# A bank for each head's scores and a raised priority for the operation that empties it, in a conv, scan and attention kernel

## The chip, the cores and the metric

The kernel runs on one core of one Trainium2 chip. A core has five engines, each with its own queue of instructions: TensorE (PE, matmuls; its weight loads are shown apart as PEld), VectorE (DVE), ScalarE (ACT), GpSimd (POOL) and SyncE (SP), which here issues most of the DMAs. PE writes its results to PSUM[...]. The metric is the device time of one execution in microseconds; the number given is the median of several runs.

## What is computed

The reference has two layers on an input of 8 images of 384 channels and 32 x 32 points (1024 tokens). Layer 0 is a normalisation, a Mamba block run forwards and backwards (a selective scan with 16 states per channel), and a gated local 3x3 convolution. Layer 1 is causal attention with six heads of 64 and a feed-forward with quantised activations. Cut to what matters:

```python
# layer 0, for both directions, and a local convolution
u = silu(conv1d(x @ in_proj)); dt, Bm, Cm = split(u @ x_proj)
delta = softplus(dt @ dt_proj + bias)
h = exp(delta * A) * h + (delta * u) * Bm        # the scan, 16 states
y = (h * Cm).sum() + u * D;  out = (y * silu(z)) @ out_proj
local = sigmoid(conv3x3(xn) + b) * xn
x = x + res_scale * (scale * (out_fwd + out_bwd) + local)
# layer 1
scores = einsum('bhqd,bhkd->bhqk', q, k); scores = where(causal, scores, -inf)
t = t + (softmax(scores) @ v) @ Wproj + bproj
t = t + ffn(layernorm(t))                        # with 8-bit quantisation by groups of images
```

The quantisation has five groups of one image each (8 images divided by five, rounded down); what lies outside the groups stays zero. So the feed-forward is computed for images 0 to 4 alone.

## The kernel before

Every tile has 128 channels or tokens on the partitions; the 384 channels are three blocks, the 1024 tokens two halves of 512, one bank each. The stages of one image are these.

- before_scan: normalisation, in projection (L341), the 1D convolution (taps on DVE at L369 for the first image, as matmuls with diagonal weights at L371 for later ones), the local convolution (`loc`, L389 and nine taps on DVE at L400), the SiLU (L434), the x projection (L487), and the "delta" step (L518 to L528: a matmul, four ACT and four DVE operations), whose results go to DRAM and are loaded again.
- The scan. It is cut into 768 units, 96 per image, of two states and 512 tokens each. For a unit POOL multiplies `g = ud * bc` (L588), ACT makes two decays `da` in PSUM (L601), DVE runs two scans (L606), POOL copies a carry (L611) and multiplies by the second row (L612), and PE transposes and adds the result into the bank `y` (L620). `g` has six buffers; POOL's first product is issued two units ahead.
- attention: projections, then for each of three pairs of heads and each block of 128 queries `scores` (below), then the transposes of the probabilities (L862), the product with the values (L875) and the rescaling (L833 to L839), and the output projection (L934).
- feed_forward: two matrix products (L992, L1036) with GELU and quantisation.

What an engine does in which order is fixed when the program is built. The scheduling layer takes the instructions in program order as their priority, gives each tile a buffer when its first instruction is placed, and puts on each engine's queue the instruction with the best priority whose inputs, by its own estimate of times, are ready. `tc.high_priority(offset=n)` gives the instructions within it a priority as if they stood n places earlier. `pin` keeps an instruction in program order on its engine. Two lists set the program order: the first image's stages alone, then slots of the scan with the preparation of the next three images spread beside them (the lists `first` and `beside`, L1121 to L1144), and after that the scan's slots with attention and feed-forward of the images done, spread by estimated durations (L1146 to L1168). The last image's attention comes at the end, alone.

Banks are tiles with a tag. `BANKS` gives each tag its number of banks, eight in all; `bank(name, tag)` takes a tile of a tag, and without a tag takes "s" and "pt" in turn (`turn`). The tag "s" has two banks. Its users are the scores, but also the preparation of the first four images (tags "s" and "pt" in turn), the projections of attention by the turn, and the feed-forward.

A pair of heads has its scores in two banks. The matmul of head 1 is issued first, that of head 0 right after it at a high priority; each uses 64 rows of the array. For each head DVE then adds the causal mask, negates, and finds the minimum along the row (L800, "the mask" below; a second short record reads the accumulated minimum `nm`), and ACT takes the exponential with `nm` as bias (L810).

Of the kernel before, what the change touches and what calls it, by code (L numbers as in the profile page):

```python
# [12 lines left out]
ALU = mybir.AluOpType  # L13
# [24 lines left out]
MASKED = -1e30  # L38
# [16 lines left out]
def kernel(  # L55
# [16 lines left out]
    nc = tc.nc  # L72
# [17 lines left out]
    def mtile(name, n=L):  # L90
        return mid.tile([P, n], F32, name=name, tag="mid")
# [1 line left out]

    BANKS = {"y": 1, "da": 2, "s": 2, "pt": 2, "av": 1}
    turn = [0]

    def bank(name, tag=None):
        if tag is None:  # L100
            turn[0] += 1
            tag = ("s", "pt")[turn[0] % 2]
        return ps.tile([P, HB], F32, name=name, tag=tag, bufs=BANKS[tag])

    def half(h):
# [2 lines left out]
    def chunk(c):  # L108
        return slice(c * P, (c + 1) * P)
# [29 lines left out]
    for d in range(2):  # L139
        nc.scalar.dma_start(out=wdt[d * DW : d * DW + RANK, :], in_=w_dt)  # L140
        nc.scalar.dma_start(
            out=wdt[d * DW + RANK : d * DW + RANK + 1, :],
# [53 lines left out]
    def binarize(src, dst, nk, nout, per, name, emit):  # L196
# [15 lines left out]
        @emit  # L212
        def _():
            st["mps"] = bank(f"mps_{name}", "av")
# [44 lines left out]
    def mean_of(c_of, name):  # L259

        m = bank(name)
        for c in range(NC):
            nc.tensor.matmul(out=m, lhsT=onesc, rhs=c_of(c), start=(c == 0), stop=(c == NC - 1))
        return m
# [42 lines left out]
    def before_scan(b, tags, emit, later=None, diags=None):  # L307
# [5 lines left out]
        def bank_of(name):  # L313
            return bank(name, next(turns))
# [359 lines left out]
    def attention(b, emit_ffn, emit):  # L674
# [83 lines left out]
        def at_once(second):  # L758
            return tc.high_priority(offset=HURRY) if second else nullcontext()

        def rows_of(e):
            return slice(e * HD, (e + 1) * HD)

        def blocks_of(n):
            return [(k0, min(k0 + HB, n)) for k0 in range(0, n, HB)]

        def probabilities(c, g, steps):


            nb = g + 1  # L770

            def scores(i, qi, n, kb, k0, k1):
                pr = mtile(f"pr_{b}_{c}_{qi}_{kb}").rearrange("p (e l) -> p e l", e=2)
                st["pr", c, g, i, kb] = pr
                if kb == 0 and i == 0:
                    for what in ("nm", "rs"):
                        st[what, c, g] = small.tile(
                            [P, QT, 2, nb], F32, name=f"{what}_{b}_{c}_{g}", tag=f"{what}{nb}"
                        )
                nm, rs = st["nm", c, g], st["rs", c, g]  # L780
                ss = [bank(f"s_{b}_{c}_{qi}_{kb}_{e}", "s") for e in range(2)]

                order = (1, 0)
                for e in order:
                    with at_once(e == order[1]):
                        mm = nc.tensor.matmul(  # L786
                            out=ss[e][:, : k1 - k0],
                            lhsT=st["q"][rows_of(e), c, chunk(qi)],
                            rhs=st["k"][rows_of(e), c, k0:k1],
                            start=True,  # L790
                            stop=True,
                        )
                    if e == order[1]:
                        pin(mm)

                w = k1 - k0
                mask = cmask[:, HB - w :] if k1 == n else cmask[:, :1].to_broadcast([P, w])
                for e in range(2):
                    x, m = pr[:, e, :w], nm[:, i, e, kb : kb + 1]
                    nc.vector.tensor_tensor_reduce(  # L800
                        out=x,
                        in0=ss[e][:, :w],
                        in1=mask,
                        scale=-1.0,
                        scalar=-MASKED,
                        op0=ALU.add,
                        op1=ALU.min,
                        accum_out=m,
                    )
                    nc.scalar.activation(  # L810
                        x, x, AF.Exp, bias=m, scale=-1.0, accum_out=rs[:, i, e, kb : kb + 1]
                    )

            for i in range(QT):
                qi = g * QT + i
                n = (qi + 1) * P
                for kb, (k0, k1) in enumerate(blocks_of(n)):
                    steps(lambda i=i, qi=qi, n=n, kb=kb, k0=k0, k1=k1: scores(i, qi, n, kb, k0, k1))
# [402 lines left out]
```

## Time and profile before

| | |
|---|---|
| median of 3 runs | 5041.66 us (5039.27 to 5051.98) |
| the profiled execution | 5052.48 us, span 5050.7 us, granted PE clock 0.883 |
| first scan of unit 0 / of unit 95 | 135.3 us / 774.3 us |
| last image's attention alone | from about 4838 us to the end |
| POOL: products L588 and L612 | 1837.9 and 1819.4 us |
| DVE: scans L606 | 907.7 and 955.1 us |
| DVE: masks L800, 576 | 298.9 us |
| PE: scores L786 | 394.6 us |

Busy time per engine in stretches of the span (us):

| stretch | PE | DVE | ACT | POOL |
|---|---|---|---|---|
| 0 to 135 | 56.05 | 89.61 | 64.39 | 13.95 |
| 135 to 215 | 47.25 | 79.38 | 48.16 | 24.07 |
| 215 to 700 | 375.02 | 395.05 | 287.76 | 378.28 |
| 700 to 840 | 100.25 | 124.68 | 81.63 | 102.13 |
| 840 to 4740 | 3212.96 | 2800.18 | 2059.06 | 3131.87 |
| 4740 to 4838 | 81.79 | 50.90 | 27.69 | 39.61 |
| 4838 to 5050 | 199.22 | 65.48 | 98.75 | 0.00 |

A profile is of one execution. In a line of instructions stand the source line, the engine, the operation, the tile written and the tiles read, and the count; an idle time is that of the engine just before the instruction, and the name behind the arrow is what ended it. A weight load and a matmul can run at the same time, so their idle times overlap too.

### The profile page before, as it was taken

The numbers are of one execution on the slowest core, as the hardware profiler recorded it, in microseconds if no ns is written. First come the engines' busy times: TensorE is split into PE (matmuls) and PEld (weight loads), VectorE is DVE, ScalarE is ACT, GpSimd is POOL, SyncE is SP. The second block draws the span as 40 slices with busy tenths as digits, with TensorE's granted clock in tenths as the row PEclk, the third lists the DMA queues.
The fourth block names the chain that finished last, engine by engine and source line by source line (L and its number), as shares of the span: only waits on it lengthen the run. The fifth ranks groups of instructions, "written<-read, shape, count | busy, mean of one in ns | idle before, by whom it ended". The sixth has DMA issues, their size and how long they took to land. (4 is left out here: it accounts for less than half of the span.)

```text
span 5050.7 us, 50731 instructions
## 1 busy us (share of the span) xinstructions
PE 4072.5 (81%) x16458; PEld 2180.7 (43%) x16458; DVE 3605.3 (71%) x4775; ACT 2667.4 (53%) x4850; POOL 3689.9 (73%) x1944
## 2 busy tenths in 40 slices
PE   4687787888888888788788888887787978978899
PEld 1243343444444444344444444443454444444444
DVE  6887988676887767786778867688766666676623
ACT  4565664564554655545656446555465355464426
POOL 0578687896868976778876688867788988888700
PEclk7788797989889889888999889998898989989999
DMA  6554546323453334463334633334533334334210
GB/s 227 204 175 160 200 155 229 109 88 118 152 187 135 119 115 154 139 200 111 103 134 143 213 111 128 110 123 155 194 132 106 118 108 143 109 101 139 88 58 26
DMA packets 365009, 696.35 MB, mean 138 GB/s; under 512 B 30104, under 2 KB 88904, under 8 KB 364744
## 3 DMA queue, kind: packets, MB, share of 16 engines
q1 hardware_dynamic: 355232, 676.97, 40.0%
q10 hardware_dynamic: 9512, 16.15, 0.9%
q8 instruction: 130, 2.13, 0.2%
q14 instruction: 135, 1.11, 0.1%
HBM read 527.33 MB, written 165.68 MB: 137 GB/s over the span
## 5 line engine op out<-in xcount | busy, mean ns | idle before, releaser
L588 POOL TENSOR_TENSOR g<-ud,bc 128x1024 f32<-128x1024 f32 x768 | 1837.9, 2393 | 654.0 <-PE y L620 523.0
L612 POOL TENSOR_TENSOR g<-g,bc 128x1024 f32<-128x1024 f32 x768 | 1819.4, 2369 | 194.9 <-DVE g L606 132.4
L601 ACT ACTIVATE da<-dl,amat 128x512 f32<-128x512 f32 x1536 | 1055.9, 691 | 1515.1 <-DVE g L606 1489.8
L606 DVE TENSOR_TENSOR_SCAN g<-da,g 128x512 f32<-128x512 f32 x768 | 907.7, 1210 | 509.6 <-POOL g L588 496.3
L606 DVE TENSOR_TENSOR_SCAN g<-da,carry,g 128x512 f32<-128x512 f32 x768 | 955.1, 1271 | 403.9 <-POOL g L588 374.5
L620 PE MATMUL y<-ident,g 128*128 128x128 f32 x6144 | 920.6, 297 | 210.3 <-POOL g L612 122.3
L620 PEld LDWEIGHTS y<-ident,g 128*128 128x128 f32 x6144 | 766.9, 153 | 644.3 <-issue 345.5
L786 PE MATMUL s<-k,q 64*128 64x512 f32 (+3 forms) x1152 | 394.6, 602 | 134.6 <-DVE nm L800 113.5
L800 DVE CUSTOM_DVE_ANT_0 pr<-s,cmask 128x512 f32<-128x512 f32 (+3 forms) x576 | 298.9, 544 | 179.3 <-PE s L786 159.9
L810 ACT ACTIVATE pr<-pr,nm 128x512 f32<-128x512 f32 (+3 forms) x576 | 348.4, 606 | 125.1 <-DVE nm L800 123.5
L862 PE MATMUL pt<-ident,pr 128*128 128x128 f32 x1728 | 302.1, 304 | 83.5 <-ACT ptn L864 38.5
L992 PE MATMUL hp<-t,w 128*128 128x512 f32 x720 | 339.3, 618 | 25.4 <-DMA w<-w1s 21.2
L1036 PE MATMUL yp<-h,w 128*128 128x512 f32 x720 | 331.9, 620 | 32.0 <-DMA w<-w2s 27.6
L341 PE MATMUL in<-xn,win 128*128 128x512 f32 x576 | 291.2, 651 | 36.5 <-DVE xc L463 15.9
L862 PEld LDWEIGHTS pt<-ident,pr 128*128 128x128 f32 x1728 | 207.0, 152 | 243.5 <-ACT ptn L864 94.3
L875 PE MATMUL av<-ptn,v 128*64 128x512 f32 (+3 forms) x1152 | 274.3, 559 | 23.2 <-DVE o L889 17.2
L611 POOL COPY carry<-g 128x2 f32<-128x2 f32 x384 | 87.7, 228 | 271.2 <-DVE g L606 271.2
L864 ACT COPY ptn<-pt 128x512 f32<-128x512 f32 (+3 forms) x576 | 254.7, 473 | 55.5 <-PE pt L862 53.5
L725 PE MATMUL qp<-t,wqk 128*128 128x512 f32 x576 | 267.8, 616 | 14.7 <-DVE t L302 12.5
L400 DVE SCALAR_TENSOR_TENSOR loc<-xn,vec,loc 128x496 f32<-128x496 f32 (+3 forms) x384 | 259.5, 722 | 20.3 <-ACT loc L389 19.0
L786 PEld LDWEIGHTS s<-k,q 64*128 64x128 f32 x1152 | 134.8, 206 | 266.5 <-DVE nm L800 190.1
L1036 PEld LDWEIGHTS yp<-h,w 128*128 128x128 f32 x720 | 141.9, 201 | 204.7 <-issue 177.2
(153 smaller groups left out, 4753.4 us busy)
## 6 DMA issues: line engine op xcount, KB each, us to landing
bc<-rows SPq DMA_DIRECT2D x512, 512.0 KB, 4.1
dl<-sdl SPq DMA_DIRECT2D x160, 256.0 KB, 2.9
ud<-sud SPq DMA_DIRECT2D x160, 256.0 KB, 2.7
t<-st SPq DMA_DIRECT2D x63, 512.0 KB, 5.1
su<-u SPq DMA_DIRECT2D x48, 512.0 KB, 3.6
du<-su SPq DMA_DIRECT2D x96, 256.0 KB, 3.8
sdl<-du SPq DMA_DIRECT2D x96, 256.0 KB, 2.9
sud<-du SPq DMA_DIRECT2D x96, 256.0 KB, 2.7
```

Source lines behind the costliest of these rows:

```text
L341: nc.tensor.matmul(out=mp, lhsT=st["win", c][:, k, i, :], rhs=st["xn"][:, k, half(h)], start=(k == 0), stop=(k == NC - 1),)
L588: pin(nc.gpsimd.tensor_tensor(g, ud, sst["bc", 0, u.b, u.part, u.n], ALU.mult))
L601: nc.scalar.activation(da, sst["dl", u.b, u.c, u.part], AF.Exp, scale=amat[:, u.c, n : n + 1])
L606: nc.vector.tensor_tensor_scan(gi[:, ::step], da[:, ::step], gi[:, ::step], first, ALU.mult, ALU.add)
L612: pin(nc.gpsimd.tensor_tensor(g, g, sst["bc", 1, u.b, u.part, u.n], ALU.mult))
L620: nc.tensor.matmul(out=y[:, j, :], lhsT=g[:, i, chunk(j)], rhs=ident, is_transpose=True, start=(u.opens and i == 0 and j == 0), stop=(u.cl ...
L786: mm = nc.tensor.matmul(out=ss[e][:, : k1 - k0], lhsT=st["q"][rows_of(e), c, chunk(qi)], rhs=st["k"][rows_of(e), c, k0:k1], start=True, st ...
L800: nc.vector.tensor_tensor_reduce(out=x, in0=ss[e][:, :w], in1=mask, scale=-1.0, scalar=-MASKED, op0=ALU.add, op1=ALU.min, accum_out=m,)
L810: nc.scalar.activation(x, x, AF.Exp, bias=m, scale=-1.0, accum_out=rs[:, i, e, kb : kb + 1])
L862: nc.tensor.transpose(pt[:, chunk(i)], pr[:, e, chunk(j % QT)], ident)
L992: nc.tensor.matmul(out=hp, lhsT=st["w1"][:, c, chunk(m % 2)], rhs=st["xn"][:, c, half(h)], start=(c == 0), stop=(c == NC - 1),)
L1036: nc.tensor.matmul(out=yp, lhsT=st["w2", k // 6][:, k % 6, :], rhs=st["h", k // NC][:, k % NC, half(h)], start=(k == 0), stop=(k == NF - 1),)
```

## The change

The tag "s" with two banks becomes two tags "s0" and "s1" with one bank each. In `scores`, head e takes its bank by name, `s0` or `s1`. Everybody else who asks for "s" gets "s0" and "s1" in turn, by a second counter. The mask operation is issued with a priority as if it stood 60 places earlier. Number of banks, operations and data are as before.

```diff
-    BANKS = {"y": 1, "da": 2, "s": 2, "pt": 2, "av": 1}
-    turn = [0]
+    BANKS = {"y": 1, "da": 2, "s0": 1, "s1": 1, "pt": 2, "av": 1}
+    turn = [0, 0]
 
     def bank(name, tag=None):
         if tag is None:
             turn[0] += 1
             tag = ("s", "pt")[turn[0] % 2]
+        if tag == "s":
+            turn[1] += 1
+            tag = ("s0", "s1")[turn[1] % 2]
         return ps.tile([P, HB], F32, name=name, tag=tag, bufs=BANKS[tag])
...
-                ss = [bank(f"s_{b}_{c}_{qi}_{kb}_{e}", "s") for e in range(2)]
+                ss = [bank(f"s_{b}_{c}_{qi}_{kb}_{e}", f"s{e}") for e in range(2)]
...
                 for e in range(2):
                     x, m = pr[:, e, :w], nm[:, i, e, kb : kb + 1]
-                    nc.vector.tensor_tensor_reduce(
-                        out=x,
-                        in0=ss[e][:, :w],
...
-                    )
+                    with tc.high_priority(offset=60):
+                        nc.vector.tensor_tensor_reduce(
+                            out=x,
+                            in0=ss[e][:, :w],
...
+                        )
```

More of the change, by code (lines that the diff above doesn't have):

```diff
@@ L799, in scores @@
                     x, m = pr[:, e, :w], nm[:, i, e, kb : kb + 1]
-                    nc.vector.tensor_tensor_reduce(
-                        out=x,
-                        in0=ss[e][:, :w],
[L803 to L808, printed above, removed]
-                    )
+                    with tc.high_priority(offset=60):
+                        nc.vector.tensor_tensor_reduce(
+                            out=x,
+                            in0=ss[e][:, :w],
+                            in1=mask,
+                            scale=-1.0,
+                            scalar=-MASKED,
+                            op0=ALU.add,
+                            op1=ALU.min,
+                            accum_out=m,
+                        )
                     nc.scalar.activation(
```

## The prediction

> **What bounds the kernel now.** I read the page first, then the waits of single engines in one stretch, then the timeline of VectorE there, and last the order of instructions of both programs. The first part of the page shows no engine near its span:
>
> ```profile
> span 5050.7 us, 50731 instructions
> PE 4072.5 (81%) x16458; PEld 2180.7 (43%) x16458; DVE 3605.3 (71%) x4775; ACT 2667.4 (53%) x4850; POOL 3689.9 (73%) x1944
> ```
>
> So what matters is which engine waits for which. The costliest groups name the scan's loop and the softmax (us busy, mean ns | idle ahead of them, and who ended it):
>
> ```profile
> L588 POOL TENSOR_TENSOR g<-ud,bc 128x1024 f32<-128x1024 f32 x768 | 1837.9, 2393 | 654.0 <-PE y L620 523.0
> L606 DVE TENSOR_TENSOR_SCAN g<-da,g 128x512 f32<-128x512 f32 x768 | 907.7, 1210 | 509.6 <-POOL g L588 496.3
> L800 DVE CUSTOM_DVE_ANT_0 pr<-s,cmask 128x512 f32<-128x512 f32 (+3 forms) x576 | 298.9, 544 | 179.3 <-PE s L786 159.9
> ```
>
> A unit of the scan takes two products on POOL, 2.39 + 2.37 = 4.77 us with the carry copy hidden, and two scans on DVE, about 2.48 us. 768 units would need 3663 us of POOL: the kernel is longer because at every point some other engine is late. Score matmuls wait for their bank (all 1152 records of L786 together), and the answer by source line gives the sum:
>
> ```profile
> its engine sat idle before it (us, times) until:
>   DVE nm L800: 303.6, 306
> ```
>
> Those 303.6 us are 190.1 of weight loads and 113.5 of matmuls (198 and 108 waits), which overlap: more than this an earlier mask can't give back. In the first 840 us another rule holds. POOL's waits between 130 and 900 us:
>
> ```profile
> POOL carry L611 <- DVE g L606: 123.5, 13, 49.0
> POOL g L612 <- DVE g L606: 39.1, 7, 18.8
> POOL g L588 <- PE y L620: 33.8, 14, 5.7
> ```
>
> and VectorE's timeline right after such a wait:
>
> ```profile
> 214.57 6.78 DVE L606 TENSOR_TENSOR_SCAN g<-da,g 128x512 f32<-128x512 f32 x6
> 221.92 2.34 DVE L606 TENSOR_TENSOR_SCAN g<-da,g 128x512 f32<-128x512 f32 x2 [0.56 <-POOL g L588]
> 226.78 2.34 DVE L606 TENSOR_TENSOR_SCAN g<-da,g 128x512 f32<-128x512 f32 x2 [2.53 <-POOL g L588]
> 231.65 2.34 DVE L606 TENSOR_TENSOR_SCAN g<-da,g 128x512 f32<-128x512 f32 x2 [2.53 <-POOL g L588]
> ```
>
> The reader should see the rhythm. While DVE works off a lump of other work (taps of the local convolution, deltas), POOL gets three units ahead and stops. After the lump three units go through DVE at once (6.78 us); from then on POOL sets the pace, 4.87 us a unit, and DVE idles 2.5 us in each. So lumps set apart by three or more empty units are worth 3 x 4.77 - 7.3 = 7.0 us each; lumps that touch share one such credit.
>
> **What the Trainium skill says.** "PSUM — Partial Sum Buffer", section "Engine vs sequencer instructions": ScalarE, VectorE and GpSimd queues are strict FIFO. The trace agrees: for 49.0 us POOL stood behind one carry copy. So an order fixed at build time is all that a priority can change. "SBUF — State Buffer", section "Who interferes with whom": a VectorE instruction with two SBUF inputs contends with a GpSimd instruction that reads SBUF. Here it does: the delta's L526 took 0.69 us with POOL stopped and 2.29 us with POOL at work:
>
> ```profile
> 353.39 2.29 DVE L526 SCALAR_TENSOR_TENSOR dp<-ew 128x512 f32<-128x512 f32 x1
> 371.66 0.69 DVE L526 SCALAR_TENSOR_TENSOR dp<-ew 128x512 f32<-128x512 f32 x1
> ```
>
> Masks and scans read one operand from PSUM and one from SBUF; masks took 0.69 us whatever POOL did, so moving them costs no contention.
>
> **The change part by part.** Nothing is computed differently; the two programs differ only in order (and in 87 table loads for 88, 1.28 us of ACT). POOL's order is the same throughout. Elsewhere 328 of 12362 matmuls stand in another place, 414 of some 4200 on DVE, 299 of 4210 on ACT, 93 of 1722 on SP.
>
> *1. The priority.* Each mask can be placed by the number of scans ahead of it on DVE. It is the same for 509 of 576 masks, lower for 11, higher for 56. A mask needs its matmul first and was put next to it already; so the priority moves hardly anything, and these waits stay. Queued behind the 56 later masks is the exp on ACT and the next score matmul on PE. One scan more is 1.25 us: 56 x 1.25 = 70 us if each were on the path, nothing if the scans that now go first pay it back (POOL waits for scans too). PE's matmuls wait for a mask in 108 of 1152 records, and POOL is 79 to 93% busy in the stretches where attention runs beside the scan, so most of it is covered. I take +3 us, between -10 and +40. In 13 of 24 rescaling steps the subtraction of L834 now follows two masks of 128 columns, 2 x 0.28 + 0.08 = 0.64 us later; 13 x 0.64 = 8 us at most, but these masks fill DVE's wait for the exponential that follows it. Within the +3.
>
> *2. A bank for each head.* Before, a pair took whichever bank came free first, so the first matmul (e = 1) always followed the earlier mask. Now head 1 always has its own; where masks run in the order 0, 1 (47 pairs) the first matmul waits for the later mask. That costs nothing: both must be there before the pair is through, and a pair issued together took 1.13 us (512 columns) against 1.73 us issued apart. Pairs whose matmuls stand next to each other: 263 of 288 before, 258 after: five times some 0.6 us, +3 us at the very most. Nothing taken.
>
> *3. The other users of the tag.* `bank(..., "s")` now alternates strictly between the two. In attention and the feed-forward the order of matmuls, evictions and loads barely moves: those of L725, L743, L992, L1036 and L934 stand where they stood against the transposes. It moves where the stages ahead of the scan run, up to unit 85 (about 711 us). This is the part with a price.
>
> *3a. The start.* Before, PE idled 12.25 us for the SiLU, then did the x projections, then the next in projection:
>
> ```profile
> 53.47 4.58 PE L487 MATMUL xp<-u,wx 128*64 128x512 f32 x8 [12.25 <-ACT u L434]
> ```
>
> Now the first half of the next in projection stands ahead of the x projections, inside that gap: its bank is freed by an ACT copy that ended about 46.6 us. The conv that follows waits for both halves, so it starts about 2.5 us sooner (six records at 0.43 us). For the third channel block two of three k steps go ahead: 1.7 us. There the sums of the weight means also move from ahead of the conv to after it (it began at 89.37 us, its input was there at 87.69): 1.7 us. Sum 5.9; the deltas that follow pass through DMAs with waits of their own, so I take -5 us (0 to -7).
>
> *3b. Units 0 to 95.* Between two units I added up the work that DVE's order puts there, by the durations of the rows in this stretch. The sum over units 0 to 94 is the same in both orders. Example, us ahead of the next unit, units 61 to 71: before 7.9, 8.8, 0.7, 26.9, 11.1, 9.6, 4.4, 0.7, 0, 0, 0; after 6.5, 2.9, 8.1, 0, 0, 0, 24.8, 5.4, 17.4, 0, 5.1. A unit takes 2.48 plus that; if this is below 4.77, the lack is taken from POOL's lead (at most 7.0), and when the lead is used up the unit takes 4.77. Before: 640.9 us for units 0 to 95; the trace has 135.3 to 774.3, 639.0, so the account holds to 0.3%. After: 626.4, that is -14.5 us, of which units 60 to 80 give -9.9 (three empty units between two lumps use up a credit that touching lumps wasted), 35 to 60 -3.9, 20 to 35 +1.5. Not in it: new waits of DVE for ACT or PE. Without any lead the account gives 0; if five of the L526 and L528 also escape POOL's reads (1.6 us each), -23. These are the bounds, and I keep -14.5.
>
> From unit 85 on the orders agree on every engine apart from the shuffles of point 1, and nothing there waits for a clock time, so an early start is carried to the end. Sum: -5 - 14.5 + 3 = -16.5 us. The profiled execution took 5052.48 us (span 5050.7 and 1.8 around it), 10.8 above the median; 5036.0/5052.5 of 5041.66 gives **5025 us**.
>
> **The rivals.** *No visible change.* What DVE wins in 3b goes to waits for ACT and PE, whose orders moved too, and only the start is left: 5041.7 - 5 = 5037. For it: DVE waited 17.5 us for the local convolution's first tap on ACT already. Against it: in units 61 to 71 DVE had hardly a wait but POOL's.
>
> *Slower by the masks.* The 56 masks behind one more scan hold up PE, whose transposes free g for POOL (523.0 us of POOL's idle time hang on that). Place: attention beside the scan; price 1.25 us each, plus what such a scan itself waits for POOL (509.6 + 403.9 us of idle time over 1536 scans, 0.6): 1.85 us. It decides from 19 masks on the path (35 - 19.5 = +15.5). With 22 of them: 41 - 19.5 = +21, 5063. For it: PE does wait for masks. Against it: a scan that goes earlier frees POOL earlier.
>
> *Much faster.* The fixed banks keep PE's pairs from waiting: half of the 113.5 us of matmuls, -57 instead of +3: 4965. Against it: 509 of 576 masks have not moved.
>
> **How the numbers follow.** 0.3% of the median, about what a measurement of this kernel tells from no change, is 15 us. Chances: my sum 0.60, no visible change 0.17, slower by the masks 0.18, much faster 0.05. My own sum with its bounds (-7 - 23 - 10 at one end, about nothing at the other: 5002 to 5040) is faster by over 15 us in four of five cases. Faster: 0.48 + 0.05 + 0.01 = 0.54; same: 0.12 + 0.16 = 0.28; slower 0.18. Below 5002 lie 0.08, above 5058 about 0.11: range 5002 to 5058; my sum's own range is 5002 to 5040.
>
> **What would show it.** Unit 95's first scan at about 755 us instead of 774.3; POOL's waits on DVE in 130 to 900 us down by some 10 us; the conv of the second channel block at about 62 us instead of 64.65. The idle time of L786 behind nm stays between 270 and 340 us, the tail from 4838 us on within 3 us of 212. Wrong if unit 95 comes at the same time, or if it comes early and the end doesn't.

## The result, and the profile after

The changed kernel takes **5076.53 us** (median of 4 runs, 5074.46 to 5083.14) against 5040.47 us of the kernel before on the same chip: ratio **1.007, 95% interval 1.0051 to 1.0089**. It is slower by about 36 us; a second comparison on another occasion, told below as e8, gave 1.0039 (1.0026 to 1.0052), 20 us. The prediction had 5025 us, and its range ended at 5058. The profiled execution has a span of 5081.0 us, 30.3 more than before.

The page of the changed kernel, with the groups that answer to those shown before (us busy, mean ns of one | idle ahead of them, and who ended most of it). Line numbers are 3 or 4 higher than before:

```profile
span 5081.0 us, 50746 instructions
...
PE 4084.7 (80%) x16458; PEld 2185.3 (43%) x16458; DVE 3608.7 (71%) x4775; ACT 2666.1 (52%) x4849; POOL 3696.0 (73%) x1944
...
L591 POOL TENSOR_TENSOR g<-ud,bc 128x1024 f32<-128x1024 f32 x768 | 1833.6, 2388 | 709.3 <-PE y L623 555.0
...
L804 DVE CUSTOM_DVE_ANT_0 pr<-s,cmask 128x512 f32<-128x512 f32 (+3 forms) x576 | 299.2, 545 | 202.9 <-PE s L789 181.7
```

No engine works much longer than before (PE 12 us more, the others within 7). What grew is idle time: POOL's ahead of its first product, 654.0 to 709.3 us, of it 523.0 to 555.0 for y on PE; and DVE's ahead of a mask, 179.3 to 202.9, of it 159.9 to 181.7 for the score that the mask reads. The score matmuls' own wait, the one that the change aims at, did not get shorter. The answer by source line for L789, 303.6 us before:

```profile
its engine sat idle before it (us, times) until:
  DVE nm L804: 322.0, 304
```

POOL's waits between 130 and 900 us of the changed kernel:

```profile
POOL carry L614 <- DVE g L609: 107.0, 13, 30.2
POOL g L591 <- PE y L623: 55.4, 17, 7.5
POOL g L615 <- DVE g L609: 34.2, 6, 12.7
```

Here is the first surprise. The waits for DVE fell by 21.4 us (162.6 to 141.2), twice what was forecast; the waits for y on PE rose by 21.6 (33.8 to 55.4). The first scan of unit 0 comes at 133.2 us instead of 135.3, that of unit 95 at 773.0 instead of 774.3, not at 755. PE's timeline where the longest wait ends that has no counterpart in the kernel before:

```profile
727.83 3.17 PE L344 MATMUL in<-xn,win 128*128 128x512 f32 x7
730.83 13.88 PE L374 MATMUL u<-up,taps 128*128 128x512 f32 x32
744.55 1.91 PE L623 MATMUL y<-ident,g 128*128 128x128 f32 x16
```

The 32 matmuls of the 1D convolution now stand in one block of 13.88 us ahead of two units' transposes, and POOL stood for the buffer that these free:

```profile
745.66 2.35 POOL L591 TENSOR_TENSOR g<-ud,bc 128x1024 f32<-128x1024 f32 x1 [6.88 <-PE y L623]
```

In the kernel before the same 32 are two blocks with a unit's transposes between them:

```profile
731.32 7.02 PE L371 MATMUL u<-up,taps 128*128 128x512 f32 x16
738.18 1.03 PE L620 MATMUL y<-ident,g 128*128 128x128 f32 x8
739.05 7.03 PE L371 MATMUL u<-up,taps 128*128 128x512 f32 x16
745.92 1.91 PE L620 MATMUL y<-ident,g 128*128 128x128 f32 x16
```

So units 0 to 95 neither won nor lost. The loss comes after them. By the first scan of each unit, the changed kernel's profile is 1.4 us early at unit 95 and 31.4 us late at unit 767, and much of that arises in short stretches where attention runs beside the scan: +5.6 in units 340 to 376, +6.4 in 628 to 666, +6.7 in 240 to 284.

### The profile page after: what moved, and what is told of

Its sections match the earlier page's. It is cut to its first block, busy times and chain, and to the rows that moved or that the text cites. A ratio compares the mean times of both kernels' runs of the same rounds, so it can differ in the third digit from the quotient of the medians.

```text
span 5081.0 us, 50746 instructions
## 1 busy us (share of the span) xinstructions
PE 4084.7 (80%) x16458; PEld 2185.3 (43%) x16458; DVE 3608.7 (71%) x4775; ACT 2666.1 (52%) x4849; POOL 3696.0 (73%) x1944
## 5 line engine op out<-in xcount | busy, mean ns | idle before, releaser
L591 POOL TENSOR_TENSOR g<-ud,bc 128x1024 f32<-128x1024 f32 x768 | 1833.6, 2388 | 709.3 <-PE y L623 555.0
L789 PE MATMUL s<-k,q 64*128 64x512 f32 (+3 forms) x1152 | 395.1, 600 | 147.1 <-DVE nm L804 124.2
L804 DVE CUSTOM_DVE_ANT_0 pr<-s,cmask 128x512 f32<-128x512 f32 (+3 forms) x576 | 299.2, 545 | 202.9 <-PE s L789 181.7
L403 DVE SCALAR_TENSOR_TENSOR loc<-xn,vec,loc 128x496 f32<-128x496 f32 (+3 forms) x384 | 263.6, 723 | 24.7 <-ACT loc L392 21.6
L789 PEld LDWEIGHTS s<-k,q 64*128 64x128 f32 x1152 | 134.2, 207 | 279.2 <-DVE nm L804 197.9
```

The costliest lines, as they stand in the source:

```text
L591: pin(nc.gpsimd.tensor_tensor(g, ud, sst["bc", 0, u.b, u.part, u.n], ALU.mult))
L789: mm = nc.tensor.matmul(out=ss[e][:, : k1 - k0], lhsT=st["q"][rows_of(e), c, chunk(qi)], rhs=st["k"][rows_of(e), c, k0:k1], start=True, st ...
```

## The experiments

The built programs tell which part of the change moves which instructions. The banks alone move 47 masks behind one more scan and two behind two more (eight stand earlier); the priority alone moves only 7 later, but it puts two masks ahead of the rescaling's subtraction (L834 before) in 13 more of the 24 cases, and moves 32 of 576 matmuls f (L847, which spread the result rs of the rescaling) and some 65 of 1728 transposes pt (L862) among the scan's transposes. The places differ too, which gave the first theory its numbers. Ratios are to the kernel before on the same chip; 0.001 is 5 us.

**e1 and e2: each part alone.**

```diff
 e1: tags "s0" and "s1" as in the change, mask without high_priority
 e2: tag "s" with two banks as before, and
+                    with tc.high_priority(offset=60):
+                        nc.vector.tensor_tensor_reduce(
```

> Only the banks: s0 and s1 as in the change, the masks at their old priority. In the trace of the changed kernel the first scan of unit 767 comes 31 us late against the kernel before; 0.7 of these arise in units 0 to 95, and after that they arise at places where one of the two parts moves instructions: +20 where the banks move them (units 226-240, 340-352, 448-462, 556-574, 628-640, 690-704), +17 where the priority does. Theory 'both parts': this kernel is slower by 20 us (17 to 25, ratio 1.0040). Theory 'the priority alone': 0 us (1.000). Theory 'the banks alone': +36 us (1.0071).

> Only the priority: the tag s with its two shared banks as before, the masks raised by 60 places. Theory 'both parts': slower by about 17 us (12 to 22, ratio 1.0034). Theory 'the priority alone': +36 us (1.0071), with PE's waits of the spread matmuls (f behind rs) up from 57 to about 77 us. Theory 'the banks alone': 0 us.

e1: 1.0022 (1.0016 to 1.0029), +11 us. e2: 1.0036 (1.0023 to 1.0049), +18 us; PE's waits of f for rs are 80.3 us. Both parts cost; e2 is as expected, e1 costs half of what the trace had suggested. The next two show why.

**e3 and e4: the banks taken apart.**

```diff
 e3 (banks, no priority; FIRST holds the scores that lie in one of the two banks before)
-        if tag == "s":
+        if tag == "s" and name[:2] == "s_":
+            tag = "s1" if name in FIRST else "s0"
+        elif tag == "s":
             turn[1] += 1
 e4 (banks, no priority)
-                for e in range(2):
+                for e in order:
                     x, m = pr[:, e, :w], nm[:, i, e, kb : kb + 1]
```

> Two banks s0 and s1, no priority. Every score tile has the bank that it had in the kernel before (a table of names), and everybody else who asks for s gets s0 and s1 in turn, as in the change. The order of masks, scores, transposes and exponentials is that of before; only units 0 to 95 and their preparation are shuffled as in the change. Prediction's account (points 3a and 3b): -19 us (0.9961). Theory 'PE takes it': DVE's waits go and POOL's waits for y on PE come in their place, as in the changed kernel's trace: -1 us (-5 to +2, 0.9998). Theory 'the early shuffle alone makes it slower': +36 us.

> The banks as in the change, no priority, and the two masks of a pair are written in the order in which their matmuls are issued, head 1 first. Then the masks run in the order 1, 0 in all 288 pairs (before: 231), and every mask, score, transpose and exponential has the place among the scans that it had before. Theory 'a fixed bank costs because head 1's matmul waits for the later mask in the pairs whose masks run 0, 1': its cost is gone, -1 us (-5 to +2, ratio 0.9998). Theory 'a fixed bank costs whatever the order': still +20 us (1.0040).

e3: 0.9974 (0.9964 to 0.9983), 13 us faster. e4: 0.9977 (0.9969 to 0.9985), 12 us faster. So the banks consist of two things: the shuffle among everybody else who uses the tag is a gain of 12 to 13 us, and the scores' fixed banks cost 23 to 24 us (1.0022 - 0.9977 and 1.0022 - 0.9974) as long as masks run in the order 0, 1 in some pairs. Turning the loop takes this whole cost away. For e3 neither theory had it right: more than the -1 us of "PE takes it", less than the -19 of the account, although its units 0 to 95 took 639.7 us, no less than before.

The rows of the masks, e1 and then e4, both with fixed banks:

```profile
L803 DVE CUSTOM_DVE_ANT_0 pr<-s,cmask 128x512 f32<-128x512 f32 (+3 forms) x576 | 299.5, 545 | 197.1 <-PE s L789 178.7
```

```profile
L803 DVE CUSTOM_DVE_ANT_0 pr<-s,cmask 128x512 f32<-128x512 f32 (+3 forms) x576 | 298.8, 544 | 182.6 <-PE s L789 163.9
```

The same work; 15 us more of DVE standing at a mask whose score isn't there. (Each row is from one execution: e1's was 6 us faster than its median, e4's 9 us slower, so the two profiles are closer to each other than the kernels are.)

Units 634 to 640 show how; they took 38.4 us in e1 and 31.6 in e4. First the order of the built programs. In e4 every pair runs 1, 0. In e1 the first two pairs of the scores that begin at unit 633 run 0, 1; from the second pair on eight masks stand one scan later than in e4 (one of them two), while the two 128-column masks behind them stand where they stood. The times show what comes of it. DVE in e1:

```profile
4039.00 0.53 DVE L803 CUSTOM_DVE_ANT_0 pr<-s,cmask 128x384 f32<-128x384 f32 x1
...
4039.46 1.22 DVE L609 TENSOR_TENSOR_SCAN g<-da,g 128x512 f32<-128x512 f32 x1
4040.59 0.53 DVE L803 CUSTOM_DVE_ANT_0 pr<-s,cmask 128x384 f32<-128x384 f32 x1
...
4046.90 0.69 DVE L803 CUSTOM_DVE_ANT_0 pr<-s,cmask 128x512 f32<-128x512 f32 x1 [0.44 <-PE s L789]
...
4049.95 0.29 DVE L803 CUSTOM_DVE_ANT_0 pr<-s,cmask 128x128 f32<-128x128 f32 x1 [2.23 <-PE s L789]
```

and PE in e1, where a record group of two is one head's matmul and of four two heads' together:

```profile
4039.60 1.57 PE L789 MATMUL s<-k,q 64*128 64x512 f32 x2 [1.76 <-DVE nm L803]
...
4041.93 2.10 PE L789 MATMUL s<-k,q 64*128 64x512 f32 x4
...
4044.80 2.07 PE L789 MATMUL s<-k,q 64*128 64x512 f32 x2
...
4047.27 1.92 PE L623 MATMUL y<-ident,g 128*128 128x128 f32 x8
```

The first matmul of the next pair waits 1.76 us for a mask. The pairs are split: one head's matmul, both together (of two different pairs), one head's again, and a single one took 2.07 us, as much as the two together at 2.10. The 128-column scores and the scan's transposes are queued behind all of it, DVE waits 2.23 us for those scores, and the scans behind that mask wait too. In e4 DVE has a wait of about the same length at the last 512-column mask, but none at the 128-column masks, whose scores are ready:

```profile
4038.11 0.69 DVE L803 CUSTOM_DVE_ANT_0 pr<-s,cmask 128x512 f32<-128x512 f32 x1 [2.35 <-PE s L789]
...
4041.78 0.29 DVE L803 CUSTOM_DVE_ANT_0 pr<-s,cmask 128x128 f32<-128x128 f32 x1
```

So one wait alone doesn't tell the two apart; the sums over units 634 to 640 do. DVE waited 5.6 us for scores in e1 and 2.3 in e4, and POOL waited four times as long for the scan's transposes. POOL's waits there, e1 (4037.86 to 4076.28 us) and then e4 (4031.72 to 4063.35 us):

```profile
POOL g L591 <- PE y L623: 9.0, 3, 4.0
```

```profile
POOL g L591 <- PE y L623: 2.2, 2, 1.9
```

Units 628 to 666 took 214.9 us in e1 and 208.0 in e4. A lower granted clock (the share of TensorE's full clock that the profile records) has a part in it: in units 634 to 640 it was 0.73 in e1 and 0.84 in e4, and PE was busy for 31.9 us instead of 27.4. It is not the whole: in units 340 to 352 e1 took 64.5 us at 0.87 and e4 60.8 at 0.86. Why the clock fell in the first of these stretches was not tested.

**e9: is the turned loop a gain of its own?** The edit of e4 in the kernel before.

> The kernel before with one edit: the two masks of a pair are written head 1 first (banks, priority and all else as before). PE's order is unchanged, DVE's and ACT's differ in which head comes first in 57 of 288 pairs. With the banks of the change this edit took the time from +10 to -11 us. Theory 'it only takes away what the fixed banks cost': 0 us here (-4 to +4, 1.000), and the -11 are those of the early shuffle. Theory 'the edit is a gain of its own': -11 us or more (0.998).

1.0003 (0.9994 to 1.0011): nothing. The edit only takes away what fixed banks cost; the -12 us of e4 are the shuffle's.

**e5: the priority.** e2, with the rescaling's operations raised as well.

```diff
+                with tc.high_priority(offset=60):
                     nc.vector.tensor_reduce(low, nm, AX.X, ALU.min)
                     nc.vector.tensor_tensor(nm, low.to_broadcast([P, QT, 2, 2]), nm, ALU.subtract)
                     nc.scalar.activation(nm, nm, AF.Exp)
...
```

> Only the priority, and the seven small operations of the rescaling (minimum, subtraction L834, exponential, products, sum, reciprocal) raised by the same 60 places as the masks. Raised alone these seven would move nothing. Here they put the subtraction ahead of the two 128-column masks again in all 24 rescaling steps (with the priority alone 13 are behind them), and 24 of the 32 spread matmuls f that had moved stand again where they stood before; the raised masks keep their places. Theory 'the masks ahead of the subtraction cost it': the priority's +17 us are gone, 0 to +5 us are left (1.0005), and PE's waits of f for rs fall from 80 back to 50 to 61 us. Theory 'the masks ahead of scans cost it': still +17 us (1.0034).

1.0004 (0.9996 to 1.0012), and f's waits for rs are 62.1 us. The priority's cost is gone although the raised masks stand behind the same scans as in e2: it lay in what the masks were put ahead of. (In the built program of e5 the two masks still stand ahead of the subtraction in three cases, as in the kernel before. The kernel before with the rescaling alone raised has every engine's order unchanged, so e5's edit is no gain of its own.) One case, units 242 and 243, DVE in e2:

```profile
1672.77 0.26 DVE L801 CUSTOM_DVE_ANT_0 pr<-s,cmask 128x128 f32<-128x128 f32 x1
...
1673.17 2.15 DVE L835 TENSOR_TENSOR nm<-low,nm 128x16 f32<-128x16 f32 x1
1675.61 2.27 DVE L837 TENSOR_TENSOR rs<-rs,nm 128x16 f32<-128x16 f32 x1 [0.28 <-ACT nm L836]
...
1678.35 1.82 DVE L840 TENSOR_TENSOR rs<-nm,low 128x16 f32<-128x16 f32 x1
```

and in e5:

```profile
1673.67 0.22 DVE L836 TENSOR_TENSOR nm<-low,nm 128x16 f32<-128x16 f32 x1
1673.81 0.28 DVE L801 CUSTOM_DVE_ANT_0 pr<-s,cmask 128x128 f32<-128x128 f32 x1
...
1674.23 1.98 DVE L838 TENSOR_TENSOR rs<-rs,nm 128x16 f32<-128x16 f32 x1
...
1676.69 2.08 DVE L841 TENSOR_TENSOR rs<-nm,low 128x16 f32<-128x16 f32 x1
```

With the subtraction first, the masks lie in the time of ACT's exponential. With the masks first nothing covers that exponential (a wait of 0.28 us in this case), and here the subtraction also met a product that POOL had just begun, POOL in e2:

```profile
1672.92 2.37 POOL L588 TENSOR_TENSOR g<-ud,bc 128x1024 f32<-128x1024 f32 x1
```

PE's f, which stands at the head of its queue, waited for the last of these operations, e2 and then e5:

```profile
1680.32 1.98 PE L848 MATMUL f<-ident,rs 128*64 128x128 f32 x16 [5.13 <-DVE rs L840]
```

```profile
1678.91 1.33 PE L849 MATMUL f<-ident,rs 128*64 128x128 f32 x10 [2.83 <-DVE rs L841]
```

Over the 21 rescalings ahead of the last image the chain from the minimum to rs took 7.54 us on average in e2 and 7.21 in e5, 7 us in sum. That is less than half of the 16 us between them. In e2 f and pt also stand elsewhere among the scan's transposes; that the rest comes from this is likely but was not shown.

**e6, e7, e8, e10: do the parts add up?** The whole change with e5's edit (e6), with e4's (e7), as it is (e8), with both (e10).

> The whole change, and the rescaling's seven operations raised by 60 places too. If the costs add up (banks +10 us as measured against the kernel before, early shuffle included; priority +17 by the subtraction's wait): +10 to +15 us against the kernel before (1.0025) instead of +36 (1.007). If the two parts of the change act only together for the rest: about +20.

> The whole change, and the masks of a pair written head 1 first. Then the banks' later masks are gone and what the priority does stays: -11 (banks with the order turned, as measured) + 17 (priority, as measured) = +6 us (1.0012) if costs add up. If the priority's cost hangs on the banks: more, up to +20.

> The changed kernel once more, on the same chip as these. Adding the parts gives +10.1 + 16.9 = +27 us; the first comparison gave +36 (1.0051 to 1.0089). Additive: 1.0054. Not additive: 1.007 again.

> The whole change with both repairs: masks of a pair written head 1 first, and the rescaling's seven operations raised by 60 places. By the sum of the parts (early shuffle -11 to -13, banks 0, priority +2): -10 us (0.998). If each repair works only while the other fault is there: between -2 and +8.

| kernel | ratio, 95% interval |
|---|---|
| e6: change, rescaling raised | 1.0022 (1.0013 to 1.0031) |
| e7: change, head 1's mask first | 1.0015 (1.0008 to 1.0022) |
| e8: change again | 1.0039 (1.0026 to 1.0052) |
| e10: change with both | **0.9963 (0.9950 to 0.9976)** |

They add up in sign and roughly in size. e6 is at e1's ratio, and e7 is near e4 plus the priority. By the parts the change should be at -13 + 24 + 17 = +28 us, 1.0056: between its two comparisons, but outside the interval of the second. e10 is at -19 us where the sum had -10, outside its interval too. So each part's cost seems to depend on the rest: the priority costs 16 us alone (e2 less e5) and 9 inside the change (e8 less e6), the fixed banks 23 to 24 us alone, 12 beside the raised masks (e8 less e7) and 30 where the rescaling is raised too (e6 less e10). In the sixteen profiles (the change and e8 are the same kernel) two marks follow the two causes:

| | with the cause | without |
|---|---|---|
| fixed banks, some masks 0, 1 (change, e1, e6, e8): DVE's idle before a mask, for its score | 178.7 to 187.8 us | 157.1 to 169.3 us |
| the same: units 340 to 376 | 201.6 to 204.6 us | 196.6 to 198.9 us |
| raised masks, rescaling not (change, e2, e7, e8): PE's idle before f, for rs | 77.5 to 82.3 us | 49.4 to 62.1 us |
| the same: units 240 to 284 | 246.5 to 249.4 us | 237.8 to 244.8 us |

**e11 to e14: where the gain of units 0 to 95 went.** e11 gives g a seventh buffer. e12, e13 and e14 keep two kinds of matmul in program order on PE: in e4's kernel, in the kernel before, and in e10's.

```diff
 e11
-        g = sp.tile([P, 2, HB], F32, name=f"g_{u.name}", tag="g", bufs=6)
+        g = sp.tile([P, 2, HB], F32, name=f"g_{u.name}", tag="g", bufs=7)
 e12, e13, e14: y of image 0, and the same for the convolution's matmul if b < 4
-                nc.tensor.matmul(
+                mm = nc.tensor.matmul(
                     out=y[:, j, :],
...
+                if u.b == 0:
+                    pin(mm)
```

> The kernel with the change's banks, no priority and head 1 first (measured -11 us), with seven buffers for g instead of six; the space is taken from the pool mid (nine buffers instead of ten), which moves masks and taps by two or three scans because the first product runs one unit further ahead. Question: do POOL's waits for y on PE (42 us in units 20 to 95, some 540 us in all) come from g's buffers? If so they fall by a third or more, units 0 to 95 take 625 us or less, and the kernel gains more than 30 us unless attention suffers from the ninth buffer. If POOL is late for other reasons: units 0 to 95 take 639 us again and the time stays within 10 us of -11.

> The kernel with the change's banks, no priority, head 1's mask first (measured -11 us, units 0 to 95 in 639.6 us), and two kinds of matmul kept in program order on PE: the transposes y of image 0's units and the diagonal matmuls of the 1D convolution of the first four images. The blocks of 20 to 32 such matmuls between two units' transposes are gone; by VectorE's order alone units 0 to 95 would take 617. Theory 'PE's order took the gain': units 0 to 95 take 617 to 628 us, POOL's waits for y in units 20 to 95 fall from 42 to under 25, and the time falls by another 11 to 22 us (0.9935 to 0.9955). Theory 'VectorE's account is wrong': 635 to 640 us again, ratio 0.9977.

> The same pins in the kernel before. VectorE's order there is as before (account 640.2 us for units 0 to 95, before 640.9). Theory 'PE's order took the gain of the changed order': little to win here, units 0 to 95 in 630 to 640 us, ratio 0.998 to 1.000. Theory 'the pins are a gain of their own': as much as in the kernel with the changed banks, 617 to 625 us.

> The change with both repairs (measured 0.9963) and the same pins. If the gains add: 0.9963 less 11 to 22 us, 0.992 to 0.994. If the pins bring nothing: 0.9963.

| | ratio, 95% interval | units 0 to 95 |
|---|---|---|
| before, e2, e5, e9 (order of before) | | 635.1 to 639.0 us |
| change, e1, e3, e4, e6, e7, e8, e10 | | 638.5 to 639.7 us |
| e11: e4 with seven g | 0.9992 (0.9985 to 0.9999) | 627.4 us |
| e12: e4, pinned | 0.9962 (0.9949 to 0.9976) | 633.4 us |
| e13: before, pinned | 0.9999 (0.9985 to 1.0012) | 636.3 us |
| e14: e10, pinned | 0.9961 (0.9949 to 0.9974) | 632.4 us |

e11 is no help: POOL's waits for y in units 20 to 95 are 45.4 us (41.6 in e4), and behind unit 95 its profile is 14 us longer than e4's; it has one buffer less in another pool there. The pins take 6 to 7 us off units 0 to 95 with the change's turns, the alternation of s0 and s1 among the other users of the tag (e12, e14), and nothing in the kernel before (e13). But they do not show what the convolution's blocks cost. The waits for y did not fall under 25 us as expected; with the blocks gone they are 49.4 us in twenty short waits instead of 41.6 in twelve. What fell in e12 are POOL's waits for DVE's scans, from 60.0 us in e4 to 48.0: the pins move 102 of DVE's operations ahead of unit 96 too, and by that order alone the account has 617 us instead of 626. So the 6 us can come from DVE's order, and the price of the blocks stays open. In the time of the whole kernel e12 is below e4 by less than their intervals tell apart, and e14 is level with e10.

## Why the prediction was wrong

The sum was -16.5 us; by the parts it is about +28, and the two comparisons had +36 and +20. Three of its terms failed: the priority, the banks and units 0 to 95. Term by term:

*Point 1, the priority: "+3 us, between -10 and +40". Measured +16* (e2 less e5). The step that failed is the sentence that 13 subtractions behind two masks cost "8 us at most, but these masks fill DVE's wait for the exponential that follows it. Within the +3." The cover was counted on the wrong side: the masks fill that wait when they come after the subtraction, as before; ahead of it they leave it bare. The 8 us are about what the chain lost on DVE (7); that f stands at the head of PE's queue, with y behind it and POOL behind y, was not priced. PE's waits of f for rs rose from 57.3 us to 80.3 in e2 and were 62.1 in e5.

*Point 2, a bank for each head: "costs nothing", "nothing taken". Measured +23 to +24* (e1 less e4, e1 less e3). This is the largest error. The wait of the first matmul for the later mask was seen and counted (47 pairs); that "both must be there before the pair is through" was wrong as a reason. It looks at the end of the one pair; but where the first matmul waits for the later mask the pair starts later, its own masks come behind one more scan, and the pairs after it inherit the delay, as in units 634 to 640 of e1. The prediction then charged the 56 later masks to the priority. 49 of them come with the banks, and e4 removes them together with the cost: 23/49 is 0.5 us for each, where the slower rival had 1.85 for those on the path.

*Point 3a, the start: -5 us, between 0 and -7. Right in size.* Unit 0's first scan came at 129.2 to 134.8 us in the eight unpinned profiles with the change's turns and six buffers for g, on average 131.9, against 136.0 in the four with the old turns. The place was wrong: the second channel block's conv began at 64.81 us, as late as before, because its second half projection still followed the x projections; the third block's conv began at 83.77 instead of 89.37.

*Point 3b, units 0 to 95: -14.5 us. Measured +2.6* (639.1 against 636.5 on average over the same eight and four). The account of DVE's order was right in direction about DVE: POOL waited 23 us less for it in units 20 to 95 of the changed kernel (85.9 to 63.2). The step that failed is that it had no PE in it: POOL's waits for y rose from 19.5 to 41.7 us there, as much as had been won. That is the rival "no visible change" in its mechanism; it was given 0.17. Why y is late was not settled: the blocks of the convolution stand ahead of it in the longest new wait, but with the pins, which take them away, y is as late. In e12 PE was busy for 377.7 of the 473.8 us of units 20 to 95.

The shuffle's gain of 12 to 13 us as a whole (e3, e4) is thus close to the -19.5 of point 3, but only 1.5 us of it are there by unit 95 (771.0 against 772.5 on average). Two further stretches are shorter in these eight profiles than in the four: units 666 to 690 by 2.4 us (134.8 to 136.2 against 137.2 to 138.2), where some transposes and output projections of the scan stand elsewhere, and the tail after unit 767 by 2.2 us on average (241.9 to 245.8 us against 245.9 to 246.2, so hardly apart). The rest lies in stretches where both programs have the same order, and where profiles of such kernels differ by several us among themselves (units 376 to 448: 458.8 to 466.9); it stays open. One thing goes with it: the less time units 95 to 767 took, the higher as a rule was their mean granted clock (0.892 and 4063 us in the change, 0.894 and 4030 in the kernel before, 0.899 and 4012 in e3, 0.902 and 4006 in e12). Which of the two follows from the other no run here separates.

The other signs: L789's waits for nm, 322.0 us, stayed in the range given (270 to 340), and the tail is within 3 us. The slower rival had the right sign and, in later masks, the right mechanism for the larger half; it named the wrong part of the change as their source, and missed the rescaling.

## What to carry to other kernels

Empty buffers with fixed owners in the order in which they are filled: with a bank for each head, the matmul that is issued first should own the bank that is emptied first, or its queue stands behind the later one (here 23 us, gone with one turned loop). Before raising one operation's priority, list what it will pass, and look for the head of a short chain that another in-order queue waits for; raise that chain with it. And an account of one engine's order gives a bound only: the gain can go to the next engine that is nearly as late, as it went here to PE.

## What the runs showed of the hardware

The rescaling's operations on 16 elements a partition, both operands in SBUF, took 0.15 to 0.18 us where POOL was not inside a product when they began (18 in the kernel before), and 1.42 us in the median where it was (54). Of these 54, 53 ended within 60 ns of the end of that product, 30 ns after it as a rule. The last, of 8.92 us, ended 40 ns after the third of the products that followed without a gap, so it stood through all four. Such an operation doesn't run slowly beside POOL, then: it ends with a product of POOL, nearly always the one that was running, and costs what is left of that. The Trainium skill's "SBUF — State Buffer", section "Who interferes with whom", says that a VectorE instruction with two SBUF inputs contends with a GpSimd instruction that reads SBUF, and calls the ports that the two share an exclusive lock; the ends of these 54 agree. It means that the price of a tiny operation depends on when it starts within POOL's 2.4 us: the subtraction shown above took 2.15 us in e2 and 0.22 in e5, half a microsecond later on the clock of its own run.
